# Where the causal mask of attention with heads of 64 is applied: from mask matmuls to a masked reduction and a select on the exponentials

## The chip, the cores and the metric

The kernel runs on one core of a Trainium2 chip. That core has five engines that run side by side, each through its own queue of instructions in order: TensorE (PE in the profile; its weight loads are PEld), VectorE (DVE), ScalarE (ACT), GpSimd (POOL) and SyncE (SP, which here only issues DMAs). They wait for each other through semaphores. The metric is the device time of one execution in microseconds; a run's time is compared as the median of several runs.

## The reference

A residual stream of 2048 tokens with 128 channels goes through four blocks. Each block is a half-weighted feed-forward layer, an attention layer and a second half-weighted feed-forward layer. The blocks differ in kind (mixture of experts, gated experts, a quantised linear layer, ternary layers). The attention layers are: heads of 16, causal; heads of 8, twice, without a mask; and in the last block 16 heads of 64, causal, with keys and values built from a latent of 64 channels:

```python
scores = jnp.einsum('bhsd,bhtd->bhst', q, k) / jnp.sqrt(jnp.float32(D))
causal = jnp.triu(jnp.full((S, S), -jnp.inf, dtype=jnp.float32), k=1)
scores = scores + causal[None, None]
probs = jax.nn.softmax(scores.astype(jnp.float32), axis=-1).astype(q.dtype)
out = jnp.einsum('bhst,bhtd->bhsd', probs, v)
```

Here the sequence is 2048 long, so a head has 2048 x 2048 scores, of which the upper triangle is masked.

## The kernel before

The program is one long stream of stages, one per layer, with all state in the on-chip memory. The order of TensorE's work is written out by hand: `pe(...)` keeps each matmul in the place where the program names it. The other engines' instructions are placed by a planner, which orders them by its own estimate of when each could start; on the chip each engine then takes its queue strictly in that order. DMAs go through SP's queue.

All attention layers run through one function, `flash` (line 970). It makes two passes over the scores of a work item, which is a group of heads and one of four blocks of 512 queries. For the heads of 64, `attn3` (line 1702) gives it 8 pairs of heads x 4 blocks of queries = 32 items, and `nh == 2`, so that `halved` is set (line 977). The heads of 16 and of 8 come with an `order` of their four heads, so that `tiled` is set (line 974).

- **First pass**, `stream_a` (line 1049). For each 128 queries (`r`) and each 512 keys (`kc`), two matmuls (line 1069), one for each head of the pair, write scores with queries on the partitions into a double bank of PSUM, of which there are two. VectorE then takes the maximum over the keys (line 1087), one reduction for both heads. Where `kc == qc` the tile lies on the diagonal (`last`) and only its first `(r + 1) * 128` columns are computed.
- **The maximum** is negated, split in two bf16 parts (`put_max`, line 1946) and brought as two further rows into the queries, so that the second pass's scores come out with it subtracted.
- **Second pass**, `stream_b` (line 1104). For each 128 keys (`kt`), four pairs of matmuls (line 1171) write scores with keys on the partitions, one bank for each head, out of three. ScalarE takes the exponential into a tile `pt` (line 1179). `on_exp` (line 1971) adds the tile to a running sum on VectorE or on GpSimd (line 1984): on VectorE for the last two key tiles of an item, otherwise the two in turn. The matmuls with the values (line 1136) are issued by `values()` one key tile later, after the next tile's scores. On the diagonal (`diag`, four key tiles of each item) only columns from `c0` on are computed.

The two passes are interleaved in one order on TensorE, the first some items ahead of the second. In between stand the projections of later items (lines 227 to 229, 1744 and 1745), whose rotation VectorE multiplies (line 1782) and GpSimd adds and splits (lines 1792 and 1798), the output projections (line 2033) and the totals of the sums (line 1997).

**The mask.** With heads of 16, the first pass adds the mask within the reduction on VectorE (line 1079) and the second lets a GpSimd select zero the masked exponentials (line 1201). With heads of 64, TensorE adds the mask: `half_masks` (line 1015) multiplies an identity with a mask of -1e30 in four bf16 matmuls of 64 rows, two for each head, and accumulates it onto the scores. It is called in the first pass at line 1074 and in the second at line 1176. Its operands are fetched by six DMAs and cast by VectorE at the stage's start (lines 1002 to 1013).

## Time and profile before

| what | value |
|---|---|
| time, median of 3 runs | 3802.96 us (3797.84 to 3808.43) |
| the profiled execution's own time | 3781.83 us |
| its span, from the first to the last instruction | 3779.9 us |
| TensorE busy, share of the span | 91% |
| VectorE, ScalarE, GpSimd busy | 76%, 54%, 22% |
| mean granted TensorE clock | 0.934 |
| first and last mask matmul start at | 2631.3 and 3629.5 us of the span |

A profile shows one execution. A line of a group names the source line, the engine, the operation, the tiles that it writes and reads, their shapes and the count, then the busy time of the group in us, the mean length of one in ns, and the idle time of the engine just before them with what ended it. A line of a timeline has the start, the length, the engine, the line and the operation, with how many were merged. "Busy" of TensorE counts a matmul from its issue to its modelled end; matmuls overlap, so that the sum of their lengths is more than the time they take, and the distance of two starts is the better measure.

### The profile page before, as it was taken

What the parts mean: (1) busy time and instruction counts of PE and PEld (TensorE: products, weight loads), DVE (VectorE), ACT (ScalarE), POOL (GpSimd) and SP (SyncE); (2) the same over time, 40 slices, a digit from 0 to 9 for tenths busy, and PEclk for the clock granted to TensorE, in tenths of its full rate; (3) what the DMA queues carried; (4) which work ended last, traced back from release to release, by engine and by line L of the source; (5) the groups of instructions that cost most, each with busy time, mean ns of one, the idle gap of its engine ahead of it and who ended that gap; (6) DMA issues with size and microseconds to landing.
All of it is one profiled execution on the core that took longest, in us unless ns stands there. A gap on an engine that the chain in (4) does not pass through costs nothing. (4 is left out here: it accounts for less than half of the span.)

```text
span 3779.9 us, 64635 instructions
## 1 busy us (share of the span) xinstructions
PE 3450.8 (91%) x25325; PEld 1847.3 (49%) x25325; DVE 2873.0 (76%) x4793; ACT 2035.4 (54%) x3838; POOL 827.9 (22%) x830
## 2 busy tenths in 40 slices
PE   7689988979999999996999999988899999999999
PEld 5543356853333333883333333376444444444458
DVE  6578556767999997668799999654677877788862
ACT  3246722315888888332688888732333444444442
POOL 1511124010000000111000000142555445533341
PEclk9779989976999999996799999898899999999999
DMA  3410023010000000102000000012443333221010
GB/s 104 94 48 19 27 69 92 1 26 5 14 10 14 8 3 1 35 7 64 9 14 6 16 5 4 12 49 75 137 147 111 99 108 97 89 63 52 24 34 12
DMA packets 124689, 170.18 MB, mean 45 GB/s; under 512 B 25120, under 2 KB 52514, under 8 KB 124384
## 3 DMA queue, kind: packets, MB, share of 16 engines
q1 hardware_dynamic: 121824, 160.80, 14.0%
q0 software_dynamic: 2560, 5.25, 0.9%
q8 instruction: 199, 3.26, 0.4%
q14 instruction: 106, 0.87, 0.1%
HBM read 101.25 MB, written 45.87 MB: 39 GB/s over the span
## 5 line engine op out<-in xcount | busy, mean ns | idle before, releaser
L1087 DVE TENSOR_REDUCE mp<-s 128x2 f32<-128x1024 f32 (+3 forms) x1440 | 1628.1, 1181 | 115.3 <-PE s L1069 84.8
L1199 ACT ACTIVATE pt<-s 128x512 f32<-128x512 f32 (+1 forms) x2368 | 1220.4, 602 | 250.5 <-PE s L1190 155.5
L1190 PE MATMUL s<-q,km 32*128 32x512 f32 (+2 forms) x2368 | 751.9, 504 | 24.2 <-ACT pt L1199 14.2
L1136 PE MATMUL pv<-pt,v 128*32 128x256 f32 (+1 forms) x8568 | 752.6, 424 | 22.9 <-ACT ov L1568 11.3
L1069 PE MATMUL s<-km,qt 32*128 32x512 f32 (+3 forms) x2368 | 634.0, 519 | 57.5 <-DVE mp L1087 36.1
L1190 PEld LDWEIGHTS s<-q,km 32*128 32x128 f32 (+1 forms) x2368 | 329.7, 188 | 549.3 <-issue 360.6
L1179 ACT ACTIVATE pt<-s 128x512 f32<-128x512 f32 (+3 forms) x640 | 306.1, 530 | 357.0 <-PE s L1171 213.8
L143 POOL TENSOR_TENSOR rs<-rs,minus_half 128x4 f32<-128x4 f32 x56 | 57.7, 1030 | 1555.9 <-DVE rs L142 1555.0
L1136 PEld LDWEIGHTS pv<-pt,v 128*32 128x32 f32 x8568 | 171.1, 109 | 325.0 <-issue 151.8
L1984 DVE TENSOR_TENSOR sum<-sum,pt 128x512 f32<-128x512 f32 (+3 forms) x328 | 259.3, 806 | 89.0 <-ACT pt L1179 87.7
L1171 PE MATMUL s<-q,k 64*128 64x512 f32 (+3 forms) x1920 | 299.9, 403 | 16.3 <-ACT pt L1179 10.8
L1136 PE MATMUL pv<-pt,latv 128*64 128x512 f32 (+3 forms) x1280 | 310.7, 565 | 1.3 <-ACT pt L1179 1.3
L1984 POOL TENSOR_TENSOR sum<-sum,pt 128x512 f32<-128x512 f32 (+1 forms) x200 | 264.8, 1324 | 182.7 <-ACT pt L1179 179.6
L1069 PEld LDWEIGHTS s<-km,qt 32*128 32x128 f32 (+1 forms) x2368 | 241.0, 195 | 119.4 <-DVE mp L1087 79.2
L1171 PEld LDWEIGHTS s<-q,k 64*128 64x128 f32 x1920 | 161.7, 188 | 226.7 <-issue 138.3
L715 ACT ACTIVATE sg<-pg 128x1024 f32<-128x1024 f32 x72 | 73.9, 1026 | 174.3 <-PE pg L229 155.3
L1069 PE MATMUL s<-k,q 64*128 64x512 f32 (+3 forms) x640 | 132.4, 428 | 19.4 <-DVE mp L1087 19.0
L1782 DVE TENSOR_TENSOR rot<-rot,tab 128x512 f32<-128x512 f32 x128 | 87.7, 685 | 74.0 <-PE rot L229 39.4
L725 PEld LDWEIGHTS pd<-l1d,h 128*128 128x128 f32 x1152 | 139.3, 192 | 5.6
L725 PE MATMUL pd<-l1d,h 128*128 128x128 f32 x1152 | 140.1, 275 | 0.0
L717 DVE TENSOR_TENSOR h<-pu,sg 128x1024 f32<-128x1024 f32 x72 | 87.9, 1220 | 60.5 <-PE pu L229 55.5
L1171 PE MATMUL s<-q,two 64*128 64x512 f32 (+3 forms) x640 | 128.3, 369 | 0.0
(575 smaller groups left out, 4682.1 us busy)
## 6 DMA issues: line engine op xcount, KB each, us to landing
tab<-in_l3rope SPq DMA_DIRECT2D x66, 256.0 KB
q<-q SPq DMA_DIRECT2D x32, 512.0 KB
k<-k SPq DMA_DIRECT2D x32, 512.0 KB
l0e<-in_l0e SPq DMA_DIRECT2D x32, 256.0 KB
q<-h SPq DMA_DIRECT2D x32, 256.0 KB
q<-rot SPq DMA_DIRECT2D x32, 256.0 KB
k<-h SPq DMA_DIRECT2D x32, 256.0 KB
k<-rot SPq DMA_DIRECT2D x32, 256.0 KB
```

The lines of the kernel that those rows point to most:

```text
L715: nc.scalar.activation(sg, pg, AF.Silu)
L717: nc.vector.tensor_tensor(h.rearrange("p m n -> p (m n)"), pu, sg, ALU.mult)
L725: nc.tensor.matmul(pd[:, i, :], h[:, m, i * P : (i + 1) * P], wd[:, m, :], start=m == 0, stop=m == 1,)
L1069: pe(nc.tensor.matmul(ps[:, o : o + w], lhsT, rhs[:, :w], start=True, stop=not masked))
L1087: ins = nc.vector.tensor_reduce(mp[:, r, j0 : j0 + 2, kc], both[:, :, :w], AX.X, ALU.max,)
L1136: i = pe(nc.tensor.matmul(pv[out_rows, lo:hi], lhsT, pts[j][:, lo:hi], start=kt == 0, stop=kt == nt - 1 and hi == CH))
L1171: pe(nc.tensor.matmul(outs[j][:, c0:], lhsT, rhs[:, c0:], start=i == 0, stop=i == len(terms[0]) - 1 and not diag,))
L1179: ex = nc.scalar.activation(pts[j][:, c0:], outs[j][:, c0:], AF.Exp, scale=scale)
L1190: pe(nc.tensor.matmul(ps[:, c0:], lhsT, rhs[:, c0:], start=i == 0, stop=i == len(terms) - 1 and (tiled or not diag),))
L1199: ex = nc.scalar.activation(pt[:, c0:], ps[:, c0:], AF.Exp, scale=scale)
L1782: nc.vector.tensor_tensor(t.bitcast(F32), ps, halves["tabs"][i], ALU.mult)
L1984: eng.tensor_tensor(t[:, c0:], other[:, c0:], pts[j][:, c0:], ALU.add)
```

## The change

The branch for `halved` masks goes: its DMAs, casts and `half_masks` with both calls. Every causal attention now does what the heads of 16 did. In the first pass, the reduction of a diagonal tile is two instructions, one for each head, which add a strip (zeros with the mask in the last 128 columns) and reduce in one go; each also reads its accumulator. In the second pass, a GpSimd select sets the exponentials above the diagonal to zero in place, in the first 128 columns of a diagonal tile; the sums and the values then use what the select leaves. `ex`, the instruction that the first value matmul waits for, is now the select.

```diff
-        if halved:
-            halves = {}
-            for name in ("ident", "maskq", "maskk"):
-                raw = pool.tile([P, 2, P], F32, name="halfraw", tag="halfraw", bufs=2)
...
-        def half_masks(outs, mask):
...
-        if tiled and causal:
+        if causal:
             junk = pool.tile([P, CH], F32, name="junk")
             strip = pool.tile([P, CH], F32, name="strip")
             nc.gpsimd.memset(strip[:, : CH - P], 0.0)
...
                                 last = causal and kc == qc
-                                masked = last and not tiled
...
-                                        ps[:, o : o + w], lhsT, rhs[:, :w], start=True, stop=not masked
+                                        ps[:, o : o + w], lhsT, rhs[:, :w], start=True, stop=True
                                     ))
                                     pos[0] += w
-                                if masked:
-                                    half_masks([ps[:, j * CH + w - P : j * CH + w] for j in range(2)], "maskq")
                                 both = ps.rearrange("p (j n) -> p j n", j=2)
                                 with tc.high_priority():
-                                    if last and tiled:
+                                    if last:
                                         for j in range(2):
                                             ins = nc.vector.tensor_tensor_reduce(
...
+        def select(t):
+            return nc.gpsimd.affine_select(
+                t, t, [[1, P]], ALU.is_ge, 0.0, base=0, channel_multiplier=-1,
+            )
...
-                                    start=i == 0, stop=i == len(terms[0]) - 1 and not diag,
+                                    start=i == 0, stop=i == len(terms[0]) - 1,
                                 ))
-                        if diag:
-                            half_masks([ps[:, c0 : c0 + P] for ps in outs], "maskk")
                         for j in range(2):
                             pts[j] = early.tile([P, CH], F32, name="pt", tag="pt", bufs=2 * nh + 2)
                             ex = nc.scalar.activation(pts[j][:, c0:], outs[j][:, c0:], AF.Exp, scale=scale)
+                            if diag:
+                                ex = select(pts[j][:, c0 : c0 + P])
```

The branch for the other heads calls the same `select` and is otherwise as it was.

More of the change, by code (lines that the diff above doesn't have):

```diff
@@ L1000, in chunks @@
             return qc + 1 if causal else NC
-        if halved:
-            halves = {}
-            for name in ("ident", "maskq", "maskk"):
-                raw = pool.tile([P, 2, P], F32, name="halfraw", tag="halfraw", bufs=2)
-                for j in range(2):
-                    nc.sync.dma_start(
-                        out=raw[P // 2 * j : P // 2 * (j + 1)],
-                        in_=a["consts"][:, slice(*CONSTS[name])].rearrange("(b i) k -> i b k", b=2),
-                    )
-                halves[name] = pool.tile([P, 2, P], BF16, name="half" + name)
-                nc.vector.tensor_copy(halves[name], raw)
-        def half_masks(outs, mask):
-            for b in range(2):
-                for j in range(2):
-                    s = slice(P // 2 * j, P // 2 * (j + 1))
-                    pe(nc.tensor.matmul(
-                        outs[j], halves["ident"][s, b], halves[mask][s, b], start=False, stop=b == 1
-                    ))
-        if tiled and causal:
+        if causal:
             junk = pool.tile([P, CH], F32, name="junk")
@@ L1191, in stream_b @@
                                 ps[:, c0:], lhsT, rhs[:, c0:],
-                                start=i == 0, stop=i == len(terms) - 1 and (tiled or not diag),
-                            ))
-                        if diag and not tiled:
-                            pe(nc.tensor.matmul(
-                                ps[:, c0 : c0 + P], masks_b["ident_b"], masks_b["maskk_b"], start=False, stop=True
+                                start=i == 0, stop=i == len(terms) - 1,
                             ))
@@ L1199, in stream_b @@
                         ex = nc.scalar.activation(pt[:, c0:], ps[:, c0:], AF.Exp, scale=scale)
-                        if diag and tiled:
-                            ex = nc.gpsimd.affine_select(
-                                pt[:, c0 : c0 + P], pt[:, c0 : c0 + P], [[1, P]], ALU.is_ge, 0.0,
-                                base=0, channel_multiplier=-1,
-                            )
+                        if diag:
+                            ex = select(pt[:, c0 : c0 + P])
                         pts[j] = pt
```

## The prediction

> **What bounds the kernel now.** I read the busy row of the page first, then the same row cut to the stretch that the change touches (attention with heads of 64, from its first mask matmul to its last), then the groups of that stretch, one piece of its timeline, and last who waits for whom.

> ```profile
> PE 3450.8 (91%) x25325; PEld 1847.3 (49%) x25325; DVE 2873.0 (76%) x4793; ACT 2035.4 (54%) x3838; POOL 827.9 (22%) x830
> ```

> ```profile
> 2630.00:3640.00 1010.00, 946.49 (x6357) 472.76 (x6357) 773.54 (x1122) 414.76 (x840) 462.06 (x350) 0.96 0.28 89
> ```

> The columns of the second line are the stretch, its length, then busy time (and instructions) of TensorE, its weight loads, VectorE, ScalarE, GpSimd. The change lies in 1010 us of the 3780. TensorE is busy 94% of it at a granted clock of 0.96, VectorE 77%, GpSimd 46% (22% over the whole span: the average hides it). So TensorE sets the pace, in an order written out by hand, and any wait at its head is lost.

> ```profile
> L1020 PE MATMUL s<-halfmaskk,halfident 64*128 64x128 bf16 x512 | 40.0, 225 | 0.0
> L1020 PE MATMUL s<-halfmaskq,halfident 64*128 64x128 bf16 x512 | 39.0, 229 | 0.0
> ```

> ```profile
> 2898.10 0.28 PE L1020 MATMUL s<-halfmaskq,halfident 64*128 64x128 bf16 x4
> 2898.29 0.19 PEld L1069 LDWEIGHTS s<-k,q 64*128 64x128 f32 x2
> 2898.29 0.44 PE L1069 MATMUL s<-k,q 64*128 64x384 f32 x2
> 2898.57 0.11 PEld L1020 LDWEIGHTS <-halfident 64*128 64x128 bf16 x4
> 2898.57 0.28 PE L1020 MATMUL s<-halfmaskq,halfident 64*128 64x128 bf16 x4
> 2898.79 0.20 PEld L1136 LDWEIGHTS pv<-pt,latv 128*64 128x64 f32 x4
> ```

> Columns: start, length, engine, line. A group of four mask matmuls holds the array for about 0.2 us: scores at 2898.29, masks at 2898.57, values at 2898.79.

> ```profile
> ACT pt L1179 <- PE s L1020: 132.7, 90, 5.4
> DVE sum L1984 <- ACT pt L1179: 90.9, 96, 3.2
> PEld s L1069 <- DVE mp L1087: 27.4, 41, 2.5
> PE s L1069 <- DVE mp L1087: 17.9, 23, 2.1
> ```

> Who waits, for whom, us in all, times, longest. ScalarE and VectorE mostly wait for TensorE; TensorE waits 45 us for VectorE's maxima.

> **What goes.** 128 first-pass and 128 second-pass groups of masks, 1024 matmuls. Their busy time (79 us) overlaps with its neighbours, so I take starts. After a second-pass score pair of 512 columns the masks start 235 ns later (median), and what follows the masks starts 216 ns after them if it uses all 128 rows (values, projections), 95 ns if it is again a 64-row pair. Without masks in between, elsewhere in the stretch, values start 320 ns after such a pair and 64-row scores 229 ns after. A group thus costs 235+216-320 = 131 ns or 235+95-229 = 101 ns. For the first pass the same rows give 318+216-404 = 130 and 318+95-310 = 103. 99 of the 250 groups recorded whole are followed by 64-row work: 0.4x101 + 0.6x131 = 119 ns. 256 x 0.119 = **-30.5 us**. Both ends: 256 x 0.095 = 24 where a wait stood behind the masks anyway, 256 x 0.216 = 55 if nothing of the group overlapped.

> At the stage's start six loads and three casts for the masks go as well. They stand ahead of the weight loads on SP's queue:

> ```profile
> 2624.98 2.69 SPq L1008 DMA_DIRECT2D halfraw<-in_consts  x4
> 2630.43 0.69 PE L1870 MATMUL fold<-l3o,l3v 64*64 64x128 f32 x4 [2.48 <-DMA l3o<-in_l3o]
> ```

> TensorE waited 2.48 us for a load issued behind 2.69 us of issues: **-2.5 us**, once (nothing to 2.7). One strip copy and one memset that come in lie beside this. Otherwise SP and ScalarE keep their order but for neighbours that swap, and so does TensorE.

> **What VectorE gets.** 128 reductions of both heads at once become 256 reductions with a mask added, each with a read of the accumulator. The attention with heads of 16 runs the same instruction:

> ```profile
> L1079 DVE CUSTOM_DVE_ANT_0 junk<-s,strip x128: 259/466/692, 188.6 to 421.6; 128x128 f32<-128x128 f32 x32, 128x256 f32<-128x256 f32 x32, 128x384 f32<-128x384 f32 x32, 128x512 f32<-128x512 f32 x32
> L1087 DVE TENSOR_REDUCE mp<-s 128x2 f32<-128x1024 f32 x224 | 268.3, 1216 | 35.9 <-PE s L1069 29.6 <-PE s L1020 6.0
> ```

> Instruction and readout end 295, 432, 565, 698 ns after their start for 128 to 512 columns. Twice that, against 411, 680, 940, 1216 ns for the one reduction, is +179 to +190, and a gap of 35 ns between the two: +0.22 us, 128 times, 28 us, VectorE from 77% to 79%. What reaches TensorE? There are two first-pass banks, so the scores two steps on wait for this reduction. In 39 of 127 diagonal steps they start less than 1 us after the reduction's end (in 25 at once), and four such steps follow each other closely, 0.88 us in sum: 39/127 x 28 = 9 us. In the changed order, 68 of the 128 pairs have other work between their halves, 26 times a 512-column sum (1.1 us), and the bank comes free only after it: +3 us, the tenth part of 26 x 1.1, since most of these sums stood ahead of the whole reduction before. **+12 us**; ends 5.5 (the 25 alone) and 31.

> VectorE's sums of diagonal tiles must now wait for the select too. 72 of its 200 diagonal sums and copies start within 0.2 us of their exponential, so these wait some 0.4 us longer, with the next maximum queued behind them. Laid along VectorE's row, its own recorded waits soon after take this up: between 0 and 2 us reach TensorE, inside the 12.

> **What GpSimd gets: the disputed cost.** 256 selects, each between an exponential and the value matmuls that read the tile. Heads of 16 show the bare step:

> ```profile
> L1201 POOL TENSOR_SCALAR_AFFINE_SELECT pt<-pt x128: 288/292/377, 211.6 to 459.7; 128x128 f32<-128x128 f32 x128
> ```

> and, among what TensorE's value matmuls of that stage waited for (us, times),

> ```profile
>   POOL pt L1201: 13.1, 31
> ```

> 67 ns from the exponential's end to the select, 292 ns, 54 ns to the matmul: 0.41 us. There TensorE waited for it at 31 of 32 diagonal key tiles, 0.42 us each, with GpSimd nearly idle. At that rate 128 diagonal tiles would cost 54 us: the upper end. Here the values are issued one key tile later, behind the next tile's scores, and start a median 2.25 us after the second exponential; only in 7 of 128 cases is that under 0.41 us. 7 x 0.41 = 3 us is the lower end, if GpSimd were idle. It isn't. It executes its queue in order, 46% busy, with

> ```profile
> L1984 POOL TENSOR_TENSOR sum<-sum,pt 128x512 f32<-128x512 f32 x168 | 231.1, 1376 | 139.5 <-ACT pt L1179 136.6
> ```

> so a select may find 1.4 us or more ahead of it, and 51 of the 128 gaps are under 1.8 us. In the changed queue many diagonal tiles stand as select, 512-column sum, select, and some selects stand behind a rotation's sum that itself waits for VectorE or ScalarE. Whoever waits: the first value matmul, behind it on TensorE everything else; on VectorE the sums above. I laid the changed GpSimd order on the recorded ends of the exponentials, gave each select 292 ns, started it no sooner than the item ahead of it ended, and shifted what follows by each stall: 38 tiles are late, 27 us in all, 13 of it in five tiles.

> [...] VectorE's 512-column sums take from 673 to 1706 ns. The select's row comes from a stage without such sums. They fill 280 of the 1010 us[...]. With 392 ns instead of 292 the same laying-out gives 43 late tiles and 34.5 us. By the row the sum is +6[...].

> **Sum.** -30.5 -2.5 +12 +34.5 = **+13.5 us**. Against the profiled execution's own time, 3781.8 us (span 3779.9), that is 3795.3. That execution lies 21 us under the median of the runs shown, so for a median I predict 3803 + 13.5 = **3816 us**, slower by 0.35%. What the measurement can tell from no change is about 0.3%, 11.4 us.

> **Rivals.** (1) *The cover holds: faster.* The half-finished bank is handed to ScalarE and VectorE some 0.2 us sooner without the masks behind it, the late tiles overlap with waits that TensorE has anyway (45 us for maxima), and only 10 us of waits are new: -33 + 10 = -23, 3780 us. For it: the median cover of 2.25 us. Against: the 51 short covers. It wins if the selects' stalls stay under some 20 us. (2) *GpSimd's queue jams: clearly slower.* A select behind a rotation whose input comes from a TensorE step behind the stalled values: GpSimd and TensorE wait on each other's order in turn. Then the rate of heads of 16 holds, 54 us, and with 12 from VectorE: -33 + 66 = +33, 3836 us. For it: five tiles already carry 13 us in my layout. Against: stalls also let GpSimd catch up. (3) *VectorE becomes the bound:* the whole 31 us and as much waiting on selects as its 72 early sums can give (72 x 0.4 = 29) reach TensorE, with 20 from the selects: -33 + 80 = +47, 3850 us. Against: at 77% it has 236 us idle in the stretch. That the masks aren't gone is no case: the changed order holds none of the 1024.

> **How the numbers follow.** Forecast 0.5, own range 3803 to 3830 (from cancelling exactly to twice the excess): half of it inside 0.3%. Rival 1: 0.27, of which 0.03 falls inside 0.3%; rival 2: 0.15; rival 3: 0.08. Faster 0.24, same 0.28, slower 0.48. The range takes in all of the forecast and what rivals 1 and 2 name, and leaves out a tenth at each end: 3778 to 3846.

> **What would show it.** In the changed profile: no line with masks, TensorE's matmul count down by 1024; 384 selects (128 before), near 300 ns[...]; a new line in the waits, value matmuls for the select, of 25 to 45 us in this stage; TensorE's wait for maxima up from 45 to near 57 us; the stretch from first to last diagonal tile longer by about 13 us, all else unchanged. The prediction is wrong if that new wait is under 15 us (rival 1) or over 50 (rival 2), or if maxima are waited for 80 us and more (rival 3).

## The result and the profile after

The changed kernel takes 3825.2 us (median of 8 runs, 3820.2 to 3838.8) against 3800.8 us of the kernel before on the same chips (8 runs): ratio 1.0059, 95% interval 1.0043 to 1.0076, or some 22 us slower. The profiled execution has a span of 3837.1 us. A second series on another chip gave 1.0050 (1.0030 to 1.0070), +19 us, with a profile of 3811.2 us; I use that one below where one profile must do, since the first lost another 27 us before it reached the attention with heads of 64 (it starts there at 2658 us, against 2631 before), where the two kernels do the same.

Busy times of the stretch with heads of 64, from its first scores to its last values, before and in the second profile of the changed kernel (the fields as in the prediction: TensorE, weight loads, VectorE, ScalarE, GpSimd, granted clock):

```profile
2631.00:3631.00 1000.00, 941.27 (x6335) 468.80 (x6333) 767.13 (x1105) 413.05 (x837) 462.06 (x350) 0.97 0.28 90
```

```profile
2635.00:3663.00 1028.00, 921.68 (x5309) 450.64 (x5310) 765.34 (x1492) 412.97 (x836) 542.17 (x606) 0.95 0.26 86
```

1024 matmuls are removed (the counts differ by 1026 between these window edges), TensorE's busy time is 20 us less, and yet the stretch is 28 us longer: TensorE's idle time went from 59 to 106 us. VectorE's busy time is the same although it has more to do (its 512-column sums got shorter, from 1116 ns in the mean to 1051 in the first profile of the changed kernel). The clock fell from 0.97 to 0.95. That clock, the third field from the end of each line, comes back in the last section.

The groups of that stretch in the first profile of the changed kernel, by shape, and who waited for the select:

```profile
L1081 POOL TENSOR_SCALAR_AFFINE_SELECT pt<-pt 128x128 f32<-128x128 f32 x256 | 83.2, 338 | 128.8 <-ACT pt L1158 127.5 <-DMA k<-k 0.5
L1054 DVE CUSTOM_DVE_ANT_0 junk<-s,strip 128x512 f32<-128x512 f32 x64 | 43.8, 684 | 13.9 <-PE s L1046 13.2
L1046 PE MATMUL s<-k,q 64*128 64x512 f32 x448 | 97.5, 453 | 30.0 <-DVE mp L1054 21.9 <-DVE mp L1062 7.9
L1117 PE MATMUL pv<-pt,latv 128*64 128x512 f32 x896 | 246.9, 630 | 9.4 <-POOL pt L1081 9.4
```

```profile
  DVE sum L1958: 80.2, 65
  PEld pv L1117: 38.0, 46
  PE pv L1117: 22.3, 26
```

The second fence answers "who waited for line 1081" in us and times. Weight load and matmul wait for the same thing, so the two PE lines overlap: all 26 matmuls waited within the wait of their weight load. That makes 46 places and 38 us, and TensorE's array itself sat idle for 22 us of them. The values wait for selects, as forecast, and VectorE's sums wait even longer: 80 us.

One such place, from the second profile (start, length, engine, line):

```profile
2847.91 0.87 ACT L1158 ACTIVATE pt<-s 128x384 f32<-128x384 f32 x2 [2.06 <-PE s L1152]
2848.59 0.29 POOL L1081 TENSOR_SCALAR_AFFINE_SELECT pt<-pt 128x128 f32<-128x128 f32 x1
2848.96 1.26 POOL L1958 TENSOR_TENSOR sum<-sum,pt 128x512 f32<-128x512 f32 x1
2850.18 0.29 POOL L1081 TENSOR_SCALAR_AFFINE_SELECT pt<-pt 128x128 f32<-128x128 f32 x1
2850.51 0.69 DVE L1958 TENSOR_TENSOR sum<-sum,pt 128x512 f32<-128x512 f32 x1 [4.43 <-POOL pt L1081]
2850.53 1.08 PE L1117 MATMUL pv<-pt,latv 128*64 128x512 f32 x4 [2.41 <-POOL pt L1081]
...
2852.33 0.68 DVE L1054 CUSTOM_DVE_ANT_0 junk<-s,strip 128x512 f32<-128x512 f32 x1
```

GpSimd had a 2.64 us pair of sums and a rotation ahead (2844.75 to 2848.64); then come select, sum, select. The second select of the tile is done at 2850.47; 0.04 us later VectorE's sum starts, 0.06 us later the values, which had waited 2.41 us. VectorE stood still for 4.43 us with a masked reduction queued behind the sum, whose second half began only at 2852.33. That is the prediction's mechanism in one picture, with more on VectorE than I had priced.

### The profile page after: what moved, and what is told of

It reads as the page before. It is cut to its first block, busy times and chain, and to the rows that moved or that the text cites. A ratio compares the mean times of both kernels' runs of the same rounds, so it can differ in the third digit from the quotient of the medians.

```text
span 3837.1 us, 63113 instructions
## 1 busy us (share of the span) xinstructions
PE 3455.6 (90%) x24301; PEld 1841.9 (48%) x24301; DVE 2866.9 (75%) x5175; ACT 2036.7 (53%) x3838; POOL 907.6 (24%) x1087
## 5 line engine op out<-in xcount | busy, mean ns | idle before, releaser
L1062 DVE TENSOR_REDUCE mp<-s 128x2 f32<-128x1024 f32 x1312 | 1528.0, 1217 | 100.0 <-PE s L1046 80.0
L143 POOL TENSOR_TENSOR rs<-rs,minus_half 128x4 f32<-128x4 f32 x56 | 57.5, 1026 | 1560.2 <-DVE rs L142 1560.0
L1958 DVE TENSOR_TENSOR sum<-sum,pt 128x512 f32<-128x512 f32 (+3 forms) x328 | 244.6, 760 | 140.7 <-POOL pt L1081 80.2
L1054 DVE CUSTOM_DVE_ANT_0 junk<-s,strip 128x256 f32<-128x256 f32 (+3 forms) x384 | 185.8, 484 | 32.2 <-PE s L1046 18.3
L1081 POOL TENSOR_SCALAR_AFFINE_SELECT pt<-pt 128x128 f32<-128x128 f32 x384 | 119.7, 324 | 320.2 <-ACT pt L1176 189.9
```

What stands on the lines that cost most here:

```text
L1054: ins = nc.vector.tensor_tensor_reduce(junk[:, :w], both[:, j, :w], strip[:, CH - w :], 1.0, NEG, ALU.add, ALU.max, mp[:, r, j0 + j, kc : ...
L1062: ins = nc.vector.tensor_reduce(mp[:, r, j0 : j0 + 2, kc], both[:, :, :w], AX.X, ALU.max,)
L1081: return nc.gpsimd.affine_select(t, t, [[1, P]], ALU.is_ge, 0.0, base=0, channel_multiplier=-1,)
L1958: eng.tensor_tensor(t[:, c0:], other[:, c0:], pts[j][:, c0:], ALU.add)
```

## The experiments

All times are against the kernel before, on the same chip; a ratio of 0.001 is 3.8 us.

**The two halves of the change, one by one.** First pass alone:

```diff
-        if tiled and causal:
+        if causal:
             junk = pool.tile([P, CH], F32, name="junk")
...
-                                masked = last and not tiled
+                                masked = False
...
-                                    if last and tiled:
+                                    if last:
```

> The first pass as in the changed kernel (masked reductions on VectorE), the second pass with its masks on the array as before. Theory (GpSimd's select is the larger part of the loss, VectorE the smaller): 128 mask groups go, -15 us, VectorE's reductions give back 12, so -3 us, within 0.3% of before. Rival A (only the select costs): -15 us, faster by 0.4%. Rival B (VectorE's 256 reductions are the loss): +15 us or more, with TensorE's wait for maxima over 80 us.

Measured: 0.9971 (0.9959 to 0.9984), -11 us.

Second pass alone:

```diff
...
-                        if diag:
-                            half_masks([ps[:, c0 : c0 + P] for ps in outs], "maskk")
...
                             ex = nc.scalar.activation(pts[j][:, c0:], outs[j][:, c0:], AF.Exp, scale=scale)
+                            if diag:
+                                ex = nc.gpsimd.affine_select(
+                                    pts[j][:, c0 : c0 + P], pts[j][:, c0 : c0 + P], [[1, P]], ALU.is_ge, 0.0,
+                                    base=0, channel_multiplier=-1,
+                                )
```

> The second pass as in the changed kernel (select on GpSimd), the first pass with masks on the array and one reduction as before. Theory: -15 us for 128 mask groups, +34 us for values that wait for selects, and part of the 52 us by which VectorE's idle time before the sums grew (selects that the sums wait for), together +25 to +35 us, slower by 0.7 to 0.9%; TensorE's wait for maxima rises over its 45 us although the reductions are those of before. Rival A: +20 us, maxima unchanged. Rival B: -10 us, faster.

Measured: 1.0022 (1.0010 to 1.0034), +8 us. Maxima are waited for as before (30 us by weight loads and 17 by matmuls; 31 and 19 over the same stretch before), against what I expected. The signs fit "the select is the loss" and rule out that the reductions are. But both sizes came out lower than the theory's, and -11 + 8 = -3 isn't the whole's +19. So the whole was run again:

> The changed kernel once more, beside the others of this call. The two halves of the change measured one by one give -11 and +8 us; the whole gave +22. If that gap is an interaction of the two, this run repeats it: ratio 1.004 to 1.008, granted clock in the stretch near 0.96. If the gap came from the lower clock of the one profiled execution (0.945 in the stretch), the ratio falls to 1.000 to 1.002.

Measured: 1.0050 (1.0030 to 1.0070), granted clock in the stretch 0.951. The result stands: the parts do not simply add up.

**What the masks cost on the array.** No mask at all inside these tiles (this run and the next two leave the second pass's mask out of the computation):

```diff
...
-                                masked = last and not tiled
+                                masked = False
...
-                                    start=i == 0, stop=i == len(terms[0]) - 1 and not diag,
+                                    start=i == 0, stop=i == len(terms[0]) - 1,
...
-                        if diag:
-                            half_masks([ps[:, c0 : c0 + P] for ps in outs], "maskk")
```

> The kernel before with no causal mask inside the diagonal tiles of the heads of 64 at all: no mask matmuls, no select, and the one reduction; the mask of these tiles is left out of the computation. It measures what the array's masks cost by themselves. By the prediction's step: 256 groups x 0.119 us + 2.5 us = -33 us, ratio 0.991. If groups mostly stood in front of waits that come anyway: -10 us, ratio 0.997. If nothing of a group overlapped: -55 us, ratio 0.986.

Measured: 0.9926 (0.9905 to 0.9947), -28 us (-20 to -36). The prediction's 33 is within it.

**Who waits for the select.**

```diff
                             if diag:
-                                ex = select(pts[j][:, c0 : c0 + P])
+                                aside = early.tile([P, P], F32, name="aside", tag="aside", bufs=2)
+                                nc.gpsimd.affine_select(
+                                    aside, pts[j][:, c0 : c0 + P], [[1, P]], ALU.is_ge, 0.0,
+                                    base=0, channel_multiplier=-1,
+                                )
```

> The changed kernel, but each select writes into a tile that nothing reads, so GpSimd does the same work and nobody waits for it; the mask of the second pass is left out of the computation. Theory (the waits for the select are the loss, not GpSimd's load[...]): -33 + 12 = -21 us against before, ratio 0.9945, 45 us faster than the changed kernel. Rival C (GpSimd's load[...] are the loss): still slower than before, +5 to +20 us.

Measured: 0.9985 (0.9969 to 1.0001), -6 us. Without values and sums that wait, the loss is gone: +19 becomes -6, so this waiting is worth some 25 us of it. But the expected -21 isn't reached. One wait is left in this run that I had overlooked: ScalarE, which may not write a tile of exponentials again before the select has read it.

```profile
ACT pt L1158 <- POOL aside L1161: 17.5, 19, 1.3
```

In this stretch of the changed kernel ScalarE never waits for the select, so this run is not quite the same work without waiters. Without any select at all:

```diff
                             ex = nc.scalar.activation(pts[j][:, c0:], outs[j][:, c0:], AF.Exp, scale=scale)
-                            if diag:
-                                ex = select(pts[j][:, c0 : c0 + P])
```

> The changed kernel without the selects; the second pass's mask of these tiles is left out of the computation. Against the run with selects that nobody reads (-6 us) it tells what GpSimd's 256 selects cost by their load[...] alone. If load is nearly free: -8 to -12 us, the same as that run within the intervals. If load matters: what costs add up to, -28 + 4 = -24 us, so load is worth 18 us.

Measured: 0.9961 (0.9942 to 0.9979), -15 us. Between this and the run before lie 9 us for GpSimd's load and ScalarE's wait together, half of the 18 of the expectation; the two intervals overlap, so that a zero isn't excluded. The planner moved little: of VectorE's 1236 instructions in the stretch (accumulator reads left out), 1187 stand in the same order with and without selects. The pair that matters is firm: with selects +19, without -15, **34 us for the selects**. And from "no masks" (-28) to this run (-15) the only addition is the masked reduction on VectorE: **13 us**.

**The interaction.** If the first pass's reductions and the selects make each other worse, one reduction without a mask should bring back more than its own 13:

```diff
...
-                                    if last:
+                                    if last and tiled:
                                         for j in range(2):
                                             ins = nc.vector.tensor_tensor_reduce(
```

> The changed kernel with the select kept, but the first pass of the heads of 64 takes one reduction without any mask: the maxima also see masked scores and are then upper bounds, which softmax allows. Theory (interaction: a sum that waits for a select stands between the two halves of a masked reduction and holds the bank, so the two costs grow together): the select's half alone, +8, less 14 us for the first pass's mask groups, -6 us, so 28 us faster than the changed kernel. Rival D (costs only add up): the changed kernel less what VectorE's reductions cost alone (4 us), about +18 us.

Measured: 1.0017 (1.0000 to 1.0033), +6 us: 13 us under the changed kernel, as much as the reductions cost without selects, and not the 28 expected. The theory of an interaction between select and masked reduction falls. What interacts is something else. This run and "second pass alone" differ only in the first pass's mask matmuls, and are the same time (+6 and +8), while without selects these matmuls are worth 20 us:

```diff
-                                masked = last and not tiled
+                                masked = False
```

> The kernel before with the first pass's masks of the heads of 64 left out (maxima as upper bounds by one reduction), the second pass masked by the array as before. By the price of a mask group: 128 x 0.119 = -15 us, and a few us for maxima that are free sooner: -14 to -20 us, ratio 0.995 to 0.996. If the masked reduction on VectorE was free anyway, it equals the run with the first pass alone, 0.997.

Measured: 0.9946 (0.9925 to 0.9968), -20 us. So beside the selects, taking these matmuls off the array brought 2 us where it brings 20 without them; each is a difference with an interval of some 8 us. This accounts for the halves that looked better than the whole: the first half's gain is not there beside the second half. That TensorE's waiting is the reason is argued; the last section has what the profiles show of it.

**Is it GpSimd's queue?** Sums moved away from the diagonal:

```diff
-                late = kt >= 4 * its[n][1] + 2
-                eng = nc.vector if late or count[0] % SHARE == 0 else nc.gpsimd
+                late = kt >= 4 * its[n][1] - 1
+                eng = nc.vector if late or count[0] % 4 == 0 else nc.gpsimd
```

> The changed kernel with GpSimd's running sums moved away from the diagonal: key tiles next to and on it are summed on VectorE, and of the others GpSimd takes three in four instead of one in two, so that it makes 216 sums instead of 224. In its queue, sums stand directly ahead of 16 selects instead of 76. Theory (selects wait behind sums in GpSimd's queue): values wait for selects 30 us or less instead of 61, time 10 to 17 us under the changed kernel, ratio 1.001 to 1.003 to before. Rival (they wait behind rotations, or the bare 0.41 us of the step itself is what costs): the wait stays at 50 us or more, ratio 1.005. If the longer sums on VectorE ahead of maxima outweigh it: slower than the changed kernel.

Measured: 1.0168 (1.0136 to 1.0199), +64 us. The waits of this kernel, us in total, times, longest:

```profile
DVE sum L1958 <- POOL pt L1081: 54.3, 57, 3.2
PEld s L1046 <- DVE mp L1054: 53.4, 37, 3.7
DVE sum L1958 <- POOL sum L1958: 46.4, 18, 4.4
PE s L1046 <- DVE mp L1054: 41.0, 28, 3.2
PEld pv L1117 <- POOL pt L1081: 17.0, 24, 3.2
...
PE pv L1117 <- POOL pt L1081: 9.0, 11, 2.8
```

That selects wait behind sums is confirmed, and the remedy refuted. With sums out of the selects' way, the values' wait falls from 61 us (38.2 by weight loads and 23.3 by matmuls) to 26. But VectorE now waits 46 us for GpSimd's crowded sums, and the stage is 43 us longer than in the changed kernel. Of the expectation's times only the last branch came true, slower than the changed kernel; the first missed by more than 50 us. I counted the sums moved, and not that they would queue up behind each other on GpSimd.

**The mask on VectorE instead:**

```diff
         def select(t):
+            if halved:
+                return nc.vector.scalar_tensor_tensor(
+                    t, cs("maskk"), 0.0, t, op0=ALU.is_ge, op1=ALU.mult
+                )
             return nc.gpsimd.affine_select(
```

> The changed kernel with the second pass's mask for heads of 64 multiplied onto the exponentials by VectorE (one instruction that compares the mask with zero and multiplies) instead of selected by GpSimd. If GpSimd's queue is what makes the select dear, values wait less than 61 us. But VectorE gets 256 x 0.32 = 82 us more, and at the share of the reductions (13 of 28) 38 us of it reach TensorE: as slow as the changed kernel, ratio 1.004 to 1.008, with the wait moved to maxima (over 150 us instead of 130). If VectorE has room in its 230 idle us: ratio 0.998 or less.

Measured: 1.0165 (1.0137 to 1.0193), +62 us. VectorE's busy time in the stretch rises from 765 to 848 us, as the 82 us of the expectation say, and values wait for VectorE's mask as they had for GpSimd's:

```profile
PEld pv L1121 <- DVE pt L1082: 41.9, 45, 3.1
...
PE pv L1121 <- DVE pt L1082: 28.7, 34, 2.6
```

So an engine with another queue is no help by itself. The step between exponential and values is dear on either; both have work of about a microsecond standing in line (in the first profile of the changed kernel, sums of 1.38 us in the mean on GpSimd, sums of 1.05 and reductions of 1.22 us on VectorE). The size was missed here too: from the run without selects (-15) to this one (+62) the mask costs 77 us, nearly all of its 82 us of work, where I had let 13/28 of it through. The wait did not move to maxima either (110 us by weight loads and matmuls, 112 in the changed kernel).

**Better than both.** The maxima need no mask: an upper bound serves the softmax as well, unless it lies so far above the true maximum that the exponentials vanish. Without a mask in either causal first pass, with the array's masks kept in the second:

```diff
...
-                                masked = last and not tiled
+                                masked = False
...
-                                    if last and tiled:
+                                    if False:
```

> The kernel before with no mask in any first pass: the heads of 64 as in the run before (-20 us), and the heads of 16 too take one reduction for two heads instead of two masked ones. 128 steps of VectorE get shorter by 0.22 us, 28 us in all; at the share that reached TensorE with heads of 64 (13 of 28) -13 us more, -33 us and ratio 0.991. If VectorE isn't what the heads of 16 wait for: -20 us, 0.9946.

Measured: 0.9924 (0.9897 to 0.9951), 3754 us against 3786, -29 us: faster than both kernels. The heads of 16 add 8 us to the 20 of the heads of 64, within the intervals of the expected 13.

**The kernel before, profiled again:**

> The kernel before, once more with a profile. The stretch of the heads of 64 ran at a granted clock of 0.965 before and at 0.945 and 0.951 in two profiles of the changed kernel. If the clock follows the kernel, this one shows 0.96 or more again; if it merely differs from execution to execution, it may be anything from 0.945 to 0.975.

Measured: 0.971 in the stretch. With two profiles of each, 0.965 and 0.971 before, 0.945 and 0.951 in the changed kernel, the lower clock goes with the kernel.

## Why the prediction was right

I forecast 3816 us, +13.5; measured are +22 and +19. The three steps of the sum came out close in size, but the waits reach TensorE in other ways than I had laid out, so that part of the hit is luck. The measured -28, +13 and +34 lead from run to run (kernel before, no masks, no selects, changed kernel); they add up to +19 by the way they are taken.

- *Masks off the array and the loads at the start, -33 us.* Measured -28 (-20 to -36). The 2.48 us that TensorE waited before the fold are gone in both changed profiles (0.0); what they are worth in time can't be told in times that spread by tens.
- *VectorE's masked reductions, +12 us.* Measured 13. Two other pairs say the same: 13 with selects (changed kernel against maxima without a mask), 9 with the second pass's masks on the array (first pass alone against maxima without a mask). Each is the difference of two series with intervals of some 5 to 8 us. The instruction took 684 ns for 512 columns (688 with heads of 16).
- *Selects, +34.5 us.* Measured 34, with an interval of some 10. I gave it all to values that wait for selects, and how late these are was right: 46 places and 38 us of waiting by weight loads, against 43 tiles and 34.5. But TensorE's own idle time before the values is only 23 us. The rest came on two other ways: VectorE's sums wait for selects (78 to 80 us), and the clock is lower (0.945 and 0.951 in the stretch, 0.965 and 0.971 before).
- *"Between 0 and 2 us reach TensorE" of the sums' waiting.* This step isn't borne out. The sums wait 78 to 80 us for selects and VectorE's idle time before them grew by some 50 us. TensorE's idle time before first-pass scores rose from 19 to 47 us (the two "PE s" lines below), with the selects and without them nearly alike (47 and 42), so that the larger part of it is the reductions, and the sums add some 4 us. That is over the 2, if not by much.
- *The length of a select.* The 34.5 us count 392 ns for each of them, 100 more than among the heads of 16. Those 100 ns were my estimate, which no trace had shown, and it was too high: a select took 338 ns in the mean and up to 803, against 294 and 377 among the heads of 16, so +44 ns. In the first profile of the changed kernel 39 of the 256 selects took over 400 ns; a sum on VectorE overlapped 28 of these, and 59 of the 211 that took 310 ns or less. No run tested whether these sums are what made the selects longer. VectorE's 512-column sums take up to 1799 ns in the profile before, not 1706. The 7.5 us that the estimate added (34.5 against 27) were right in sum by chance.
- *What the profile would show.* No mask line, 1024 matmuls fewer, 384 selects: as said. The stretch grew by 28 us, not 13, and two of my signs of being wrong came up. With weight loads and matmuls added, as I had counted, values waited 61 us for selects (25 to 45 forecast, over 50 a sign of rival 2) and scores 112 us for maxima (57 forecast, 80 a sign of rival 3). The count was at fault: a weight load and its matmul wait for one thing, and in the run without selects 105 us of such waits for maxima cost 13 us of time. TensorE's idle time is the better measure, 23 and 47 us.

The waits of the second profile of the changed kernel (us, times, longest):

```profile
PEld pv L1117 <- POOL pt L1081: 38.2, 46, 3.4
PE s L1046 <- DVE mp L1054: 33.3, 27, 3.5
...
PE pv L1117 <- POOL pt L1081: 23.3, 28, 3.0
...
PE s L1046 <- DVE mp L1062: 13.3, 12, 2.5
```

The same count misled me on the heads of 16. Their 13.1 us in 31 waits are not 31 of 32 tiles:

```profile
  PEld pv L1136: 9.7, 22
  PE pv L1136: 3.5, 9
```

The 9 matmuls waited with their weight loads, so 22 tiles waited, 0.30 us for each of the 32 and not 0.42. The 38.2 us over 128 tiles here are 0.30 us as well: with sums ahead of the selects, the longer cover of a whole key tile brought the wait no lower.

Rival 1, that the cover holds, would have needed stalls under some 20 us and a gain. Rival 2's 54 us for the selects lie outside the 34 and its interval; selects did stand behind other work in GpSimd's queue, as the run with the sums moved shows. Rival 3 is excluded by the run without selects: the reductions alone leave the kernel 15 us faster than before.

What stays open: how much of the 34 us is load and how much waiting (9 and 25 by two runs whose intervals overlap), and what of the lost gain of the first pass's mask matmuls the clock doesn't explain.

## What to carry to other kernels

What a step between an exponential and its matmul costs depends on the queue it is put in, not on its length alone: two selects of 0.3 us for each of 128 tiles cost 34 us, with sums of 1.3 us standing ahead of them in GpSimd's queue, and the same mask on VectorE, no longer in itself (0.32 us, from 83 us more of VectorE's busy time for 256 of them, against a select's mean of 338 ns), cost 77. Before moving a mask to another engine ask whether it is needed: a maximum that only has to bound the scores needs none, and that was worth 29 us. And halves of a change that are measured one by one needn't add up when both act on what one engine waits for.

## What the runs showed of the hardware

I had expected a microsecond of waiting on TensorE to cost a microsecond. Here it seems to have cost more, for a lower granted clock followed such waits (0.50 instead of 1.00). The stretches that follow the place shown above, in the second profile of the changed kernel (start:end, length, then busy times by engine and, third from the end, the clock):

```profile
2845.00:2849.00 4.00, 3.11 (x19) 1.50 (x17) 1.04 (x5) 1.73 (x4) 3.84 (x5) 1.00 0.07 24
2849.00:2852.40 3.40, 1.08 (x4) 0.20 (x4) 1.90 (x5) 0.00 (x0) 1.47 (x2) 1.00 0.26 84
2852.40:2855.80 3.40, 3.19 (x14) 1.94 (x16) 3.33 (x11) 1.28 (x3) 3.22 (x5) 0.50 0.38 131
2855.80:2859.20 3.40, 3.19 (x17) 1.72 (x14) 3.40 (x6) 1.60 (x4) 1.73 (x4) 0.50 0.49 154
2859.20:2862.60 3.40, 3.40 (x14) 1.50 (x13) 3.22 (x5) 0.00 (x0) 2.98 (x4) 0.50 0.62 178
2862.60:2866.00 3.40, 3.40 (x25) 2.16 (x23) 2.47 (x4) 1.86 (x4) 1.45 (x2) 0.99 0.75 266
```

In the 3.4 us before 2852.4 TensorE was busy for 1.08; then it ran at half the clock for 10.2 us, in which it was busy for 94 to 100% of the time; a matmul of 128x512 took 0.63 us there (2853.06) instead of 0.40 (2843.16).

The measure is a count over these two profiles, which hold 541 windows of 3.41 us at full rate. After the 496 in which TensorE idled for less than 1.0 us the clock never dropped, after the 18 with 1.7 us or more it dropped each time, after the 27 between 11 times. It came back 30 times, each time after a window with 0.21 us of idle time or less.

In sum the stretch ran at half rate for 69 and 59 us in the two profiles before, 114 and 100 in those of the changed kernel, 79 without selects, and 174 with the sums moved, which was the slowest. So the changed kernel has 21 to 35 us more at half rate than the run without selects; if all of it were matmuls bound by the clock, half of it would be lost, by this estimate 11 to 18 of the selects' 34 us. The busy times agree. The run without selects has this line:

```profile
2623.00:3618.00 995.00, 910.23 (x5309) 444.78 (x5309) 777.43 (x1489) 412.73 (x837) 467.87 (x353) 0.96 0.28 90
```

Against it the second profile of the changed kernel (1028.00 and 921.68) is 33 us longer with the same matmuls: 11 us more of TensorE's busy time and 22 us more of its idle time.

The clock may also have a part in the gain that the first pass's mask matmuls do not bring beside selects. Without selects, leaving them out took 20 to 24 us off TensorE's busy time (941 and 937 to 917) and 7 to 17 off the half rate (69 and 59 to 52). With selects ("second pass alone" against the changed kernel with one reduction without a mask) it took 9 us off the busy time (926 to 917), while the half rate rose from 76 to 102 us and the idle time by 8. The runs after leaving them out have one profile each.

That the waits cause the clock is read from the order in time in these profiles; no run took the one away and kept the other.
